# A planned order for a four-layer graph network: transfers planned later than their data, a re-cut tail, and new seeds

## The chip, the cores and the metric

The kernel runs on one core of a Trainium2 chip. The metric is the device time of one execution in microseconds (us). The engines are PE (matrix multiplication; the loading of its weights has a row of its own, PEld), DVE (vector), ACT (scalar, activations), POOL (GpSimd) and SP, which here does nothing but issue DMA transfers. Each engine works through its own list of instructions in order and waits on semaphores for the others.

## The reference

The input is x, 64 graphs of 256 nodes with 128 features (float32), and one 256 x 256 adjacency matrix. Four layers follow one another, and after each the result is added to x and layer-normalized over the features:

```python
# layer 0: five gated recurrent steps; adj @ h is both m_in and m_out
u3 = h @ u3_w.T + u3_b
z = sigmoid(av @ w3_w.T + w3_b + u3);  r = sigmoid(av @ w4_w.T + w4_b + u3)
hv = tanh(av @ w5_w.T + w5_b + (r * h @ u5_w.T + u5_b))
h = (1.0 - z) * h + z * hv
# layer 1: a masked softmax over edges, split into its diagonal and the rest
out = (A * M) @ (x @ W[0]) + (A * (1.0 - M)) @ (x @ W[1]) + bias
# layer 2: graph attention (softmax over masked scores), layer norm, then a GIN block
h_gat = relu(layernorm((softmax(scores) * adj) @ h))
z = relu(layernorm(((1 + eps) * h_gat + adj @ h_gat) @ W1 + b1))
out = relu(z @ W2 + b2 + h_gat)
# layer 3: a polynomial in adj of degree three, with seven weight matrices
y = sum_k (adj^k @ x) @ V_k
```

## The kernel before

The graphs are taken in 32 pairs. A pair's x is one tile of 128 partitions by 512 numbers (two graphs, two blocks of 128 nodes, 128 features). For every pair the program records operations: an engine or a choice of engines, an estimated time for each, what is read, what is written. `pe`, `act`, `dve`, `pool` and `S.add` record; nothing is issued until all 32 pairs are recorded.

`Schedule.order` (from line 164) then plays the whole list through in time, with one clock per engine, and issues the operations in the order of their planned starts. This order is what the chip gets: each engine's list, SP's too, is in that order, and the semaphores only make late data wait. The planner picks, among all operations whose inputs are planned to be there, the one that can start first; on equal starts the one that is most overdue by `late`. Three things in it matter here.

- `SEEN` and `LAG` say how long after an operation's end another engine can see its result. A transfer's own duration is in its `dma` triple: wait, move, after. Loads of x and of transposed x have `XLOAD` and `TLOAD`.
- Buffers are shared by class (`CLASSES`): 15 tiles of class X for x, 4 of class T for transposed x as it is loaded (`hT`), 38 of class A for everything else of this size, 8 PSUM banks and so on. A tile goes back to `free` when its last reader is planned to be done, and the planned start of the next user is not before that. `hT` of a pair is read in the first of the five steps alone, last by the instruction of line 769.
- `SEEDS` holds a number for each window of 15 us of planned time. A number other than 0 shifts the `late` of every operation by a pseudo-random amount, and so deals a different order among operations that compete in this window.

A turn (line 558) transposes a tile through DRAM: DVE transposes blocks of 32 x 32 (line 578), SP writes the tile out (line 580), and SP fetches it back with four transfers (line 586). Each costs SP an issue, and every layer has turns: 315 in all, five of them per pair in layer 0. Lines 595 and 599 are the same for the last step of layer 0. In layer 2 a row of scores goes out and comes back in the same way (lines 853 and 854), `store` (line 908) writes the result, and `load` (line 299) reads x and transposed x for later pairs.

Products with the adjacency are made by `spread7` (lines 628 to 649), which trades an eighth of the multiplications for sums on DVE and POOL; layer 3 has similar forms in `polynomial7` (line 1014) and `spread_on7` (line 1057). Gates of layer 0 are matmuls of 512 columns (lines 746 to 762). At the very end, `plain` and `by_tile` choose forms with shorter chains.

`by_tile` (lines 944 to 968) is layer 3 of the last pair. It multiplies the four blocks of tokens into one bank r, copies r to rr, multiplies four tiles t of their own, adds a2T (adjacency squared) times rr to each, and calls `finish` for tiles 0 and 1 together, then for 2, then for 3. `finish` (lines 970 to 991) takes the mean of squares of a tile (ACT with an accumulator, line 976; for the second tile of a pair DVE, lines 980 and 981), adds epsilon (DVE, line 984), raises to the power -1/2 (POOL, line 985), scales the tile (lines 987 and 988) and stores it (line 991). Means need no subtraction, since the weights are centred beforehand.

Of the kernel before, what the change touches and what calls it, by code (L numbers as in the profile page):

```python
# [9 lines left out]
ALU = mybir.AluOpType  # L10
AX = mybir.AxisListType

P = 128
# [47 lines left out]

SLOW = (1.3, 1.1, 1.4, 0.8)

SEEDS = [0, 113, 303, 1481, 0, 12107, 0, 23552, 32642, 38944, 40117, 45598, 51141, 55839, 63359, 69543, 72829,
         79574, 82143, 87571, 0, 98805, 103528, 113912, 114624, 0, 126288, 133041, 139576, 144350, 0, 153924, 0,
         162906, 171850, 173442, 179398, 188820, 193760, 197487, 201873, 206536, 212282, 216407, 222763, 227951,
         233844, 242079, 243498, 250362, 255262, 263475, 269522, 271926, 278854, 283108, 287499, 292248, 301945,
         304995, 0, 0, 0, 0, 0, 0, 0, 0, 0, 0, 0, 0, 0, 0, 14340575, 14343728, 14346224, 0, 14354974, 0, 14360087,
         14365526, 14369726, 14372687, 0, 0, 14385549, 14386751, 14392959, 14396499, 0, 14402025, 14408122,
         14412300, 14417102, 14417543, 14421809, 14425091, 0]  # L70


def mm(cols, n=1):

    return n * (0.2241 if cols <= 130 else cols * 0.001665 + 0.0065)
# [40 lines left out]
class Schedule:  # L116
# [47 lines left out]
    def order(self, tiles):  # L164

        self.prepare()
        engines = dict.fromkeys([*SEEN, "PORT"], 0.0)
        free = {cls: [(0.0, k) for k in range(len(ts))] for cls, ts in tiles.items()}
        ready, full, moved, out, window = [op for op in self.ops if not op.before], set(), 0.0, [], 0

        def slots(v):
            return [s for s in free[v.cls] if not v.seeded or (v.cls, s[1]) in full]

        while ready:
            best, homes, seed = None, {}, SEEDS[window] if window < len(SEEDS) else 0
            for op in ready:
                held = op.since
                for v in op.holds:
                    if v.home is None:
                        if (v.cls, v.seeded) not in homes:  # L180
                            homes[v.cls, v.seeded] = min((s for s, _ in slots(v)), default=1e9)
                        held = max(held, homes[v.cls, v.seeded])
                if held == 1e9 or best and held > best[0][0]:
                    continue
                way = None
                for engine, us, uses, spare, fn in op.plans:
                    start = max(held, *(engines[e] for e in uses))
                    if way is None or start + us + spare < way[0]:
                        way = start + us + spare, start, engine, us, uses, fn
                late = op.late  # L190
                if seed and op.pair >= 0:
                    late += NUDGE * (1 + seed % 3) * shuffled(op.number, seed)
                    late += GROUP * (seed // 3 % 3) * shuffled(100000 + 4 * op.pair + op.layer, seed)
                key = (way[1], late, op.number)
                if best is None or key < best[0]:
                    best = key, op, way
            if best is None:
                raise RuntimeError("the shared tiles are too few for this order")
            (start, _, _), op, (_, _, engine, us, uses, fn) = best
            if start >= (window + 1) * WINDOW:  # L200
                window += 1
                continue
            ready.remove(op)
            for v in op.holds:
                if v.home is None:
                    slot = min(slots(v), key=lambda s: s[0])
                    free[v.cls].remove(slot)
                    v.home, v.ap = slot[1], tiles[v.cls][slot[1]]
            end, base = start + us, engine.rstrip("+-")
            for e in uses:  # L210
                engines[e] = end
            seen = SEEN[base] + LAG
            if op.dma:
                wait, move, after = op.dma
                moved = max(moved, end + wait) + move * MARGIN
                seen = moved + after - end + LAG
            out.append((start, op.number, op, fn))
            for v in op.holds:
                v.left, v.end = v.left - 1, max(v.end, end + seen)
                if not v.left:  # L220
                    free[v.cls].append((v.end, v.home))
                    (full.add if v.full or v.seeded else full.discard)((v.cls, v.home))
            for x in op.then:
                same = engine != "SP" and x.base == base
                x.waits, x.since = x.waits - 1, max(x.since, end + (AGAIN.get(base, 0.0) if same else seen))
                if not x.waits:
                    ready.append(x)
        self.span = max(engines.values())
        return [(op, fn) for _, _, op, fn in sorted(out, key=lambda x: x[:2])]
# [11 lines left out]
def kernel(ctx: ExitStack, tc: tile.TileContext, x, xT, adj, adjT, mats, cols, rows, out):  # L241
# [11 lines left out]
    def pe(us, fn, r, w):  # L253
        S.add([("PE", us, fn)], r, w)

    def act(us, fn, r, w):
        S.add([("ACT", us, fn)], r, w)
# [289 lines left out]
    def tokens(v):  # L547
        return v.at(4, D)
# [395 lines left out]
    def by_tile(xT, qT, p):  # L944

        r, rr, tiles = bank(), Value("A", name="rr"), []

        def product(t, o, c, k):
            def fn():
                nc.tensor.matmul(o(), tokens(xT)[:, c, :], vx.ap[:, k, :], start=(k == 0 or c == 0), stop=False, skip_group_check=True)  # L950
                nc.tensor.matmul(o(), tokens(qT)[:, c, :], vq.ap[:, k, :], start=False, stop=True, skip_group_check=True)
            pe(mm(128, 2), fn, [xT, qT, vx, vq, *[t] * (k == 1 and c > 0)], [t])

        for c in range(4):
            product(r, lambda c=c: tokens(r)[:, c, :], c, 1)
        evacuate(lambda: rr.at(512), lambda: r.at(512), [r], [rr])
        for c in range(4):
            t = bank()
            product(t, lambda t=t: t.at(D), c, 0)
            tiles.append(t)  # L960
        for group in ((0, 1), (2,), (3,)):
            for c in group:
                def fn(c=c, t=tiles[c]):
                    for j in range(2):
                        nc.tensor.matmul(t.at(D), a2T.ap[:, j, c % 2 * P:(c % 2 + 1) * P], tokens(rr)[:, c - c % 2 + j, :], start=False,
                                         stop=(j == 1), skip_group_check=True)
                pe(mm(128, 2), fn, [a2T, rr, tiles[c], *tiles[max(c - 1, 0):c]], [tiles[c]])
            finish([tiles[c] for c in group], Value("A", name="last"), group[0], p)

    def finish(ts, o, first, p):  # L970

        n, s, st, junk = len(ts), Value("S", name="ms"), Value("S", name="st"), Value("A", name="junk")
        mv = lambda k: s.at(32)[:, 2 * k:2 * k + 2]
        var, rs = (lambda: s.at(32)[:, 1:2 * n:2]), (lambda: s.at(32)[:, 8:8 + n])
        means, outs = [Part(s) for _ in ts], [Part(o) for _ in ts]
        act(0.37, lambda: nc.scalar.activation(junk.at(D), ts[0].at(D), AF.Square, scale=D ** -0.5, accum_out=mv(0)[:, 1:2]),
            [ts[0]], [means[0], junk])

        def by_dve():
            nc.vector.bn_stats(st.at(6), ts[1].at(D))  # L980
            nc.vector.bn_aggr(mv(1), st.at(6))
        if n > 1:
            dve(0.5, by_dve, [ts[1]], [means[1], st])
        dve(0.07, lambda: nc.vector.tensor_scalar(rs(), var(), LN_EPS, None, op0=ALU.add), means, [s])
        pool(0.7, lambda: nc.gpsimd.tensor_tensor(rs(), rs(), neg_half.ap[:, :n], op=ALU.pow), [s, neg_half], [s])
        if n > 1:
            act(0.35, lambda: nc.scalar.mul(o.at(n, D)[:, 0], ts[0].at(D), rs()[:, 0:1]), [ts[0], s], [outs[0]])
        dve(0.3, lambda: nc.vector.tensor_scalar(o.at(n, D)[:, n - 1], ts[n - 1].at(D), rs()[:, n - 1:n], None, op0=ALU.mult),
            [ts[n - 1], s], [outs[n - 1]])
        where = out[2 * p:2 * p + 2].rearrange("b (t p) d -> p (b t) d", p=P)[:, first:first + n]  # L990
        S.add([("SP", 0.52, lambda: nc.sync.dma_start(where, o.at(n, D)))], outs, [], (0.6, 0.25 * n, 0.9))
# [144 lines left out]
```

## Time and profile before

| | us |
|---|---|
| median of three runs | 1469.06 (1468.51 to 1469.07) |
| profiled execution | 1470.28 |
| its span, first to last instruction | 1468.5 |
| PE busy | 1458.2 |
| DVE busy | 1277.1 |
| ACT busy | 1067.8 |
| POOL busy | 990.8 |

The span is 1.8 us shorter than the execution that it belongs to, and that execution is 1.2 us longer than the median. Engine rows are times in which at least one instruction of the engine ran. Matmuls overlap, so PE's row can count a short stall as busy; the distance from one matmul's start to the next is the finer measure. The granted clock of PE is 1.00 in all stretches that the prediction uses. A float32 matmul stands in the trace as two instructions. "SPq" is SP's queue: the time from an issue to the next, or a wait in front of one.

### The profile page before, as it was taken

The page shows a single profiled execution, that of the slowest core. Times are in us where ns is not written, and L with a number is a line of the kernel's source. Part 1 is how long each engine was busy: PE and PEld are TensorE (multiplying, and loading weights), DVE is VectorE, ACT ScalarE, POOL GpSimd, SP SyncE. Part 2 cuts the span into 40 slices and gives each one's busy share as a digit, 9 for nine tenths or more (in the row PEclk, how much of TensorE's full clock was granted, in tenths as well). Part 3 has the DMA queues.
Part 4 walks back from the last instruction along what each step waited for, and adds up shares of the span by engine and source line. Part 5 has one row for each costly group of instructions (what it writes and reads, how often), then busy time and mean ns, then how long its engine had stood idle before and what let it go on. Part 6 is the DMA issues. An engine that isn't in the chain of part 4 may idle for free.

```text
span 1468.5 us, 29324 instructions
## 1 busy us (share of the span) xinstructions
PE 1458.2 (99%) x8188; PEld 1064.8 (73%) x8188; DVE 1277.1 (87%) x3166; ACT 1067.8 (73%) x3277; POOL 990.8 (67%) x1549
## 2 busy tenths in 40 slices
PE   9999999999999999999999999999999999999998
PEld 6555666666677777777676777777777767788998
DVE  7866978988899989989998989888798998999986
ACT  4444555666787988887876677767678787899986
POOL 4432454466677878787684767766677776789764
PEclk9999999999999999999999999999999999999999
DMA  7554455676778898888778575876767878787763
GB/s 228 102 120 95 101 115 130 146 160 148 155 155 173 177 187 177 172 167 162 150 154 164 125 157 127 170 148 136 152 141 169 155 156 161 161 164 168 155 131 75
DMA packets 901283, 219.83 MB, mean 150 GB/s; under 512 B 673280, under 2 KB 892544, under 8 KB 901120
## 3 DMA queue, kind: packets, MB, share of 16 engines
q1 hardware_dynamic: 901120, 217.96, 70.9%
q8 instruction: 66, 1.08, 0.3%
q14 instruction: 97, 0.79, 0.2%
HBM read 118.43 MB, written 99.42 MB: 148 GB/s over the span
## 4 chain that ended last, share of the span: by engine, by line
PE 94%; DVE 2%; POOL 2%; SPq 1%; issue 1%; DMA 0%; ACT 0%; POOLq 0%; DVEq 0%; ACTq 0%
PE ps L628 24%; PE ps L761 9%; PE ps L746 9%; PE ps L762 9%; PE ps L747 9%; PE ps L754 9%; PE ps L784 7%; PE ps L1014 6%; PE ps L884 4%; PE ps L1057 2%; PE ps L844 2%; PE ps L610 1%; PE ps L1040 1%; SPq L586 1%; PE ps L799 0%
## 5 line engine op out<-in xcount | busy, mean ns | idle before, releaser
L628 PEld LDWEIGHTS ps<-aT,a 128*128 128x128 f32 x2192 | 296.3, 192 | 84.0 <-issue 74.4
L274 ACT COPY a<-ps 128x128 f32<-128x128 f32 (+2 forms) x612 | 255.7, 437 | 112.0 <-PE ps L628 52.2
L628 PE MATMUL ps<-aT,a 128*128 128x128 f32 x2192 | 322.6, 275 | 1.1 <-DVE a L634 0.7
L750 ACT ACTIVATE a<-ps,bzrh 128x512 f32<-128x512 f32 x160 | 110.7, 692 | 107.5 <-PE ps L747 103.2
L765 ACT ACTIVATE ps<-ps,bzrh 128x512 f32<-128x512 f32 x160 | 106.6, 666 | 88.5 <-PE ps L762 87.2
L643 POOL TENSOR_TENSOR a<-a 128x256 f32<-128x256 f32 x139 | 107.2, 774 | 93.1 <-ACT a L274 90.4
L761 PE MATMUL ps<-a,w 128*128 128x512 f32 x320 | 163.8, 594 | 0.1
L762 PE MATMUL ps<-a,u5h 128*128 128x512 f32 x320 | 163.4, 592 | 0.0
L747 PE MATMUL ps<-a,w 128*128 128x512 f32 x320 | 163.4, 592 | 0.0
L754 PE MATMUL ps<-a,w 128*128 128x512 f32 x320 | 162.6, 593 | 0.1
L649 DVE TENSOR_TENSOR a<-ps,a 128x256 f32<-128x256 f32 x237 | 98.0, 416 | 73.9 <-PE ps L628 34.5
L707 ACT ACTIVATE a<-ps 128x128 f32<-128x128 f32 x502 | 132.8, 289 | 33.1 <-PE ps L784 21.2
L647 POOL TENSOR_TENSOR a<-a 128x128 f32<-128x128 f32 x206 | 99.6, 489 | 65.4 <-DVE a L643 55.2
L715 POOL TENSOR_TENSOR s<-s,neg_half 128x4 f32<-128x4 f32 x127 | 137.7, 1086 | 6.1
L756 ACT ACTIVATE a<-ps,bzrh 128x512 f32<-128x512 f32 x160 | 110.5, 691 | 39.0 <-PE ps L754 36.3
L784 PE MATMUL ps<-W,a 128*128 128x128 f32 x960 | 135.2, 275 | 0.0
L784 PEld LDWEIGHTS ps<-W,a 128*128 128x128 f32 x960 | 123.7, 192 | 13.8 <-issue 12.0
L746 PE MATMUL ps<-a,W 128*128 128x512 f32 x256 | 131.1, 594 | 0.5 <-DVE a L649 0.5
L578 DVE STREAM_TRANSPOSE a<-a 128x512 f32<-128x512 f32 x185 | 128.2, 698 | 2.5 <-ACT a L727 0.5
L747 PEld LDWEIGHTS ps<-a,w 128*128 128x128 f32 x320 | 60.8, 190 | 76.5 <-issue 67.0
L762 PEld LDWEIGHTS ps<-a,u5h 128*128 128x128 f32 x320 | 60.8, 190 | 76.5 <-issue 64.3
L767 DVE SCALAR_TENSOR_TENSOR ps<-a,ps 128x512 f32<-128x512 f32 x160 | 109.2, 683 | 3.8 <-ACT a L756 2.8
(268 smaller groups left out, 3588.1 us busy)
## 6 DMA issues: line engine op xcount, KB each, us to landing
e<-a SPq DMA_DIRECT2D x283, 256.0 KB
a<-e SPq DMA_DIRECT2D x1132, 64.0 KB
e<-b SPq DMA_DIRECT2D x32, 512.0 KB
b<-e SPq DMA_DIRECT2D x128, 128.0 KB
x<-x_in SPq DMA_DIRECT2D x32, 256.0 KB
t<-xT_in SPq DMA_DIRECT2D x32, 256.0 KB
a<-d SPq DMA_DIRECT2D x32, 256.0 KB
y_out<-a SPq DMA_DIRECT2D x31, 256.0 KB
```

Of the source, the lines that this page charges most:

```text
L274: S.add([("ACT", us[0], lambda: nc.scalar.copy(o(), i())), ("DVE", us[1], lambda: nc.vector.tensor_copy(o(), i()))], r, w)
L578: dve(n / 512 * 0.55 + 0.09, lambda: nc.vector.transpose(st.at(n), i.at(n)), [i], [st])
L628: pe(mm(128), lambda: nc.tensor.matmul(blk(t, k), left(), rt(), start=start, stop=True, skip_group_check=True), [*r, right, terms, *[t] * ...
L707: nc.scalar.activation(tokens(junk)[:, c, :], v.at(len(tiles), D)[:, k, :], AF.Square, scale=D ** -0.5, accum_out=mv()[:, c, 1:2])
L715: pool(1.02, lambda: nc.gpsimd.tensor_tensor(rs(), rs(), neg_half.ap, op=ALU.pow), [s, neg_half], [s])
L746: nc.tensor.matmul(t.at(512), mat("u3"), hT.at(512), start=True, stop=False)
L747: nc.tensor.matmul(t.at(512), w4.ap, mT.at(512), start=False, stop=True)
L750: act(0.59, lambda t=t, r=r: nc.scalar.activation(r.at(512), t.at(512), AF.Tanh, bias=bzrh.ap[:, 1:2], scale=0.5), [t, bzrh], [r])
L754: pe(mm(512), lambda t=t, mT=mT: nc.tensor.matmul(t.at(512), w3.ap, mT.at(512), start=False, stop=True, skip_group_check=True), [w3, mT, t ...
L761: nc.tensor.matmul(t.at(512), w5.ap, mT.at(512), start=True, stop=False)
L762: nc.tensor.matmul(t.at(512), u5h.ap, r.at(512), start=False, stop=True)
L784: nc.tensor.matmul(tokens(t)[:, c, :], tokens(i)[:, c, :], w(), start=(first and k == c == 0), stop=(k == len(lefts) - 1), skip_group_chec ...
```

## The change

Four things are changed.

1. Planning of transfers: an operation of SP that follows another engine's is planned `QUEUED` = 0.5 us later than before.
2. Planning of tiles: a tile of class T counts as free 4.0 us later than its last reader's planned end.
3. `SEEDS` is replaced as a whole (the first two numbers are equal); the order of issue differs throughout.
4. The tail: in `by_tile` the a2T products of tiles 0 and 1 come before the products of tiles 2 and 3, and each later tile's own a2T product comes directly after its product. In `finish` a tile that is alone no longer has its epsilon added by DVE: tiles 2 and 3 have one more column, which a memset sets to sqrt(128 * epsilon), and ACT's sum of squares over 129 columns contains it. The two-tile case is as before, but for the planner's time of the add (0.15 for 0.07).

```diff
+QUEUED, SLACK = 0.5, {"T": 4.0}
...
-SEEDS = [0, 113, 303, 1481, 0, 12107, 0, 23552, 32642, 38944, 40117, 45598, 51141, 55839, 63359, 69543, 72829,
...
+SEEDS = [0, 113, 201, 0, 6923, 12557, 17576, 0, 28432, 33733, 41075, 46356, 54499, 57205, 61367, 69244, 73096,
...
-                    free[v.cls].append((v.end, v.home))
+                    free[v.cls].append((v.end + SLACK.get(v.cls, 0.0), v.home))
...
-                x.waits, x.since = x.waits - 1, max(x.since, end + (AGAIN.get(base, 0.0) if same else seen))
+                more = AGAIN.get(base, 0.0) if same else seen + (QUEUED if x.base == "SP" and base != "SP" else 0.0)
+                x.waits, x.since = x.waits - 1, max(x.since, end + more)
...
-        def product(t, o, c, k):
+        def product(t, o, c, k, after=()):
...
-            pe(mm(128, 2), fn, [xT, qT, vx, vq, *[t] * (k == 1 and c > 0)], [t])
+            pe(mm(128, 2), fn, [xT, qT, vx, vq, *after, *[t] * (k == 1 and c > 0)], [t])
...
         for c in range(4):
             t = bank()
-            product(t, lambda t=t: t.at(D), c, 0)
+            if c > 1:
+                dve(0.1, lambda t=t: nc.vector.memset(t.at(D + 1)[:, D:], (D * LN_EPS) ** 0.5), [rr], [t])
+            product(t, lambda t=t: t.at(D), c, 0, [tiles[-1]] if c > 1 else [])
             tiles.append(t)
-        for group in ((0, 1), (2,), (3,)):
-            for c in group:
-                def fn(c=c, t=tiles[c]):
+            for k in {1: (0, 1), 2: (2,), 3: (3,)}.get(c, ()):
+                def fn(k=k, t=tiles[k]):
                     for j in range(2):
...
-                pe(mm(128, 2), fn, [a2T, rr, tiles[c], *tiles[max(c - 1, 0):c]], [tiles[c]])
-            finish([tiles[c] for c in group], Value("A", name="last"), group[0], p)
+                pe(mm(128, 2), fn, [a2T, rr, tiles[k]], [tiles[k]])
+            if c:
+                finish(tiles[:2] if c == 1 else tiles[c:], Value("A", name="last"), max(c, 2) if c > 1 else 0, p)
...
-        act(0.37, lambda: nc.scalar.activation(junk.at(D), ts[0].at(D), AF.Square, scale=D ** -0.5, accum_out=mv(0)[:, 1:2]),
-            [ts[0]], [means[0], junk])
...
         if n > 1:
+            act(0.37, lambda: nc.scalar.activation(junk.at(D), ts[0].at(D), AF.Square, scale=D ** -0.5, accum_out=mv(0)[:, 1:2]),
+                [ts[0]], [means[0], junk])
...
-        dve(0.07, lambda: nc.vector.tensor_scalar(rs(), var(), LN_EPS, None, op0=ALU.add), means, [s])
+            dve(0.15, lambda: nc.vector.tensor_scalar(rs(), var(), LN_EPS, None, op0=ALU.add), means, [s])
+        else:
+            act(0.37, lambda: nc.scalar.activation(junk.at(D + 1), ts[0].at(D + 1), AF.Square, scale=D ** -0.5, accum_out=rs()),
+                [ts[0]], [s, junk])
```

## The prediction

> **What bounds the kernel now.** I read the page first, then the windows by stage, the waits of PE and of SP, the chain around each PE stall, and the timeline of the end.
>
> ```profile
> span 1468.5 us, 29324 instructions
> PE 1458.2 (99%) x8188; PEld 1064.8 (73%) x8188; DVE 1277.1 (87%) x3166; ACT 1067.8 (73%) x3277; POOL 990.8 (67%) x1549
> PE 94%; DVE 2%; POOL 2%; SPq 1%; issue 1%; DMA 0%; ACT 0%; POOLq 0%; DVEq 0%; ACTq 0%
> ```
>
> PE is busy for all but 10.3 us, and the chain is 94% PE. But a busy PE could hide slack, so I checked its pitch in the chain (start, length, line, count):
>
> ```profile
> 1139.97 0.86 PE ps L746 x2
> ...
> 1443.70 0.89 PE ps L1014 x8
> ...
> 1456.42 1.73 PE ps L936 x8
> ```
>
> Two instructions of 512 columns take 0.86 us, 8 of 128 take 0.89, 8 of 256 take 1.73: pitches of 0.429, 0.1117 and 0.216. The groups by shape count 6284 instructions of 128 or 130 columns, 292 of 256 and 1600 of 512 (12 others are tiny): 6284 x 0.1117 + 292 x 0.216 + 1600 x 0.429 = 1451 us. PE runs at its pitch nearly everywhere, and the change leaves the list of matmuls as it is. So only about 17 us can move. By the starts of the matmul records, where each start-to-start time is set against its pitch, they are: 1.2 before the first matmul, 3.5 more in the first 40 us, 6.5 of stalls between 40 and 1450, 5.3 from the start of the last matmul to the end (the remainder is rounding of the pitches).
>
> The windows show where the 6.5 us lie (columns: window, length, then busy time of PE, PEld, DVE, ACT, POOL, clock, DMA share, GB/s):
>
> ```profile
> 40.00:500.00 460.00, 460.00 (x2187) 299.50 (x2186) 385.56 (x864) 294.85 (x773) 259.00 (x417) 1.00 0.65 135
> 500.00:600.00 100.00, 99.12 (x604) 75.36 (x603) 88.93 (x244) 86.62 (x286) 80.40 (x122) 1.00 0.86 175
> 1100.00:1200.00 100.00, 99.36 (x567) 72.17 (x566) 91.74 (x221) 80.92 (x256) 74.23 (x117) 1.00 0.80 162
> 1300.00:1400.00 100.00, 98.29 (x692) 88.90 (x691) 94.52 (x288) 93.47 (x358) 82.31 (x115) 1.00 0.79 160
> ```
>
> From 40 to 500 PE never stops. Start to start the stalls are 1.8 us at 548 to 570, 1.85 at 1107 to 1184 and 2.75 at 1330 to 1400. Their causes differ. The first is a late transfer; its chain runs through the SP queue, back to back, to a tile that lands late, then POOL:
>
> ```profile
> 550.43 1.90 SPq L586
> 556.63 2.10 DMA a<-e
> 558.80 0.74 POOL a L634
> ```
>
> The other two have no transfer at their root. At 1155 DVE and POOL sit on each other: DVE L643, 0.42 us at its usual length, starts in its record at 1155.14 and is through only at 1158, when POOL's last sum ends:
>
> ```profile
> 1155.14 2.97 DVE L643 TENSOR_TENSOR a<-a 128x256 f32<-128x256 f32 x2 [0.21 <-ACT a L274]
> ...
> 1156.74 0.74 POOL L1004 TENSOR_TENSOR a<-a 128x256 f32<-128x256 f32 x1
> ```
>
> At 1396 POOL runs L1005, L1004, L1006 and then the L634 for which PE waits 1.6 us. So 1.8 of the 6.5 us belong to transfers, 4.7 to engines.
>
> SP's own waits, which the new planning aims at (total, times, longest):
>
> ```profile
> SPq L580 <- DVE a L578: 149.4, 92, 8.0
> SPq L586 <- DMA e<-a: 52.3, 39, 3.5
> SPq L299 <- DVE a L769: 39.8, 13, 11.3
> ```
>
> SP stands still for hundreds of us, and PE hardly notices: prefetch and many pairs in flight hide it.
>
> **The change part by part.**
>
> *The tail.* Today, in the last pair, 16 products of r run from 1457.98, 16 of the tiles from 1459.77, 16 with a2T from 1461.55 to 1463.34 (0.1117 each). The finish is then:
>
> ```profile
> 1463.51 1.73 POOL L985 TENSOR_TENSOR s<-s,neg_half 128x2 f32<-128x2 f32 x3 [2.44 <-DVE s L984]
> 1463.54 0.28 ACT L976 ACTIVATE a<-ps 128x128 f32<-128x128 f32 x1
> 1463.71 0.20 ACT L976 ACTIVATION_READ_ACCUMULATOR a<-ps 128x1 f32 x1
> ...
> 1465.28 0.35 DVE L988 TENSOR_SCALAR a<-ps,s 128x128 f32<-128x128 f32 x1 [0.17 <-POOL s L985]
> ```
>
> Three powers in a row on POOL (0.70, 0.52, 0.53) set the end: the last one's input is there at 1464.09, but POOL is free only at 1464.73. The new order puts a2T of tiles 0 and 1 before the products of 2 and 3: 8 instructions, 0.89 us, earlier. The first group's power then begins about 0.9 us earlier, at 1462.61 (with its add as now), and ends at 1463.31; tile 2's ends at 1463.83. The last tile's matmuls still end at 1463.34, its square at 1463.91. The removed DVE add (L984, 0.15 and the hand-over) brings the last power to 1463.97, its end to 1464.50, the scaling to 1464.52 to 1464.87, against 1465.63: 0.76 earlier. What follows (SP issue and landing, 2.9 to the span's end) stays. The cover at risk: a2T of tile 0 now comes 0.89 earlier, at 1460.66, and its input, ACT's copy of r, ends at 1460.55. That is 0.1 of room; behind a waiting a2T the whole rest of PE's work queues, so a copy that starts 0.5 later costs 0.4. And ACT runs six L727 until 1462.25, which can hold the first square; that would put the last power 0.15 later. I take 0.7, ends 0.2 and 0.8. The two new memsets of one PSUM column are not in this trace: between 0.06 (the memset of neg_half) and 0.35 (L988) each, in DVE's idle 2.68 us before L980, so nothing; uncovered they delay the square of tile 2, which has 0.3 of room before POOL takes it. A square of 129 columns for 128 is nothing.
>
> *Half a microsecond before SP issues.* 381 issues follow an engine's result: 283 + 32 first halves of a turn, 32 score lines, 34 stores. Each is planned 0.5 us later, and what reads the turned tile with it. No instruction is added; the queue's order and the margin change. 92 waits on L578 average 1.6 us, so 0.5 shortens the blocking in front of the queue by up to 46 us of SP time, and PE's consumers get about 0.5 more room. The only transfer stall begins with 0.48 us of lateness (558.2) and pulls 1.3 more after it through DVE and POOL. I take all of it, 1.8; the ends are 0 and 1.8. Each pair has 12 such steps, so it lives some 6 us longer in the plan; some 15 pairs in flight hide that. Without that cover it would cost up to 6 once, at the end.
>
> *Four microseconds for tiles of transposed x.* 28 of 32 loads reuse one of four tiles. From the eighth load on the issue precedes the first matmul that reads it by 65 to 255 us, so four is nothing. But the fifth to seventh go out at 22.4, 23.7 and 36.4 for matmuls at 37.6, 39.8 and 42.3: leads of 15.2, 16.0 and 6.0. I take nothing, because PE has pairs 0 to 3 to work on; the upper end is 4 for each of two turnovers, 8. The SP time it saves (39.8 us of blocking) lies at 25 and 44 for the most part, where PE is full: nothing.
>
> *New seeds, a new order.* The 4.7 us that engines cause are dealt anew. Nothing in the change speaks to them, so I take them as unchanged; ends: 0 and twice as much. The start: the first two seeds (0 and 113) are unchanged, and no early load follows a computed value, so 0.
>
> [...]
>
> Sum against the profiled execution (1470.28, span 1468.5, 1.8 around it): -0.7 - 1.8 = -2.5, so a span of 1466.0. That execution is 1.2 above the median of 1469.06; the same difference gives **1466.6**. 0.2%, 2.9 us, is about what a measurement of this kernel can tell from no change.
>
> **Rivals.**
> 1. *Nearly every stall goes.* For it: 460 us in a row without one. Against: two of three places have no transfer in them. All 6.5 and the tail give 1461.9; with an eighth or so left, 1463.
> 2. *The transfers were hidden anyway.* SP's 149 us of waits cost PE 0.3 us directly ("PE ps L628 <- DMA a<-e: 0.3, 1, 0.3" is among PE's waits), and a new order makes another late tile. Only the tail counts: 1468.4.
> 3. *The start starves (slower).* The loads at 22 to 36 us go out 4 us later, and pairs 4 to 6 with them; the next generation 4 more. If PE has nothing else in 20 to 120 us, it loses 8: 1469.06 - 0.7 + 8 = 1476.4. It decides from 3.6 us uncovered. For: a lead of 6.0. Against: PE full there with SP blocked for 11.3 us at 25.
> 4. *Transfers pass each other badly (slower).* A first half that is planned later falls behind another tile's four fetches (L586, 0.55 each, 2.2). Less the 0.5 of room, PE loses 1.7 each time; four such among 315 turns make 1469.06 - 0.7 + 6.8 = 1475.2. It decides from the third. For: the DMA share of 0.86 at 500 to 600. Against: one such case today.
>
> **How the numbers follow.** Forecast 0.37 (own range 1465.0 to 1468.2), rivals 0.22, 0.17, 0.12 and 0.12. Faster than 1466.1: a third of the forecast (0.12) and rival 1 (0.22), 0.34. Slower than 1472.0: rivals 3 and 4, 0.24. Within: 0.42. The range goes from just under rival 1 to rival 3, 1462.5 to 1476.5, which leaves the full end of rival 1 and more than 8 us of loss outside, some 2 in 10.
>
> **What would show it.** Right: the last L985 starts within 0.1 us of its square's end, the last scaling 1.2 to 1.4 us after the last a2T instruction; "SPq L580 <- DVE a L578" well under 149; no PE wait on a transfer. PE at 100% in 40 to 120 speaks against rival 3. Wrong: stalls over 10 us between 40 and 1450, on whatever engine they end; or PE idle over 6 us in the last 20, if pairs came to the end in another order.

## The result and the profile after

The changed kernel takes **1478.55 us** (median of six runs, 1476.45 to 1480.64) against 1469.07 (six runs, 1468.18 to 1469.82): a ratio of 1.0064, interval 1.0053 to 1.0074. It is slower, outside the range of 1462.5 to 1476.5. Its profiled execution took 1477.63, with a span of 1475.9, 7.4 above that of before. The page of the changed kernel:

```profile
span 1475.9 us, 29402 instructions
PE 1460.9 (99%) x8188; PEld 1064.6 (72%) x8188; DVE 1283.8 (87%) x3154; ACT 1061.4 (72%) x3284; POOL 1007.2 (68%) x1559
```

The matmuls are the same 8188, so all 7.4 us are stalls or ends. Set start to start against the pitch, as in the prediction, they are:

| us of stall | 0 to 40 | 40 to 100 | 500 to 600 | 700 to 800 | 1000 to 1200 | 1200 to 1300 | 1300 to 1400 | 1400 to 1450 | all | last matmul's start to end |
|---|---|---|---|---|---|---|---|---|---|---|
| before | 2.84 | 0.13 | 1.79 | -0.03 | 1.66 | 0.10 | 2.71 | -0.01 | 8.98 | 5.28 |
| after | 2.77 | 2.13 | 1.34 | 0.75 | 0.97 | 0.24 | 8.12 | 0.37 | 16.52 | 5.09 |

(The stretches that are left out hold -0.2 in all in both; values below 0.15 are rounding of the pitches. The prediction's figures for before, 3.5 up to 40 us and 6.5 from there to 1450, come out here as 2.8 and 6.1.) 7.54 of stalls less 0.19 at the tail make the 7.35. The same stages in the windows of after (columns as in the prediction's fence):

```profile
40.00:100.00 60.00, 58.12 (x211) 33.20 (x210) 50.99 (x98) 26.17 (x47) 27.09 (x46) 1.00 0.50 106
500.00:600.00 100.00, 99.32 (x615) 76.08 (x615) 93.62 (x255) 84.03 (x276) 82.81 (x119) 1.00 0.88 175
1100.00:1200.00 100.00, 99.51 (x566) 71.79 (x565) 90.67 (x223) 77.21 (x248) 76.33 (x119) 1.00 0.75 153
1300.00:1400.00 100.00, 94.70 (x657) 83.58 (x657) 93.60 (x271) 87.10 (x333) 77.72 (x109) 1.00 0.79 163
```

Two stages carry the loss: 40 to 100, where PE of before was full, and 1300 to 1400, where its busy time falls from 98.29 to 94.70. The granted clock is 1.00 in all four. Lines of after are numbered three to eight higher (L583 is the old L580, L753 the old L750). Waits of PE in after:

```profile
PE ps L757 <- ACT a L753: 2.9, 3, 1.9
PE ps L813 <- DVE ps L807: 1.5, 1, 1.5
PE ps L613 <- DVE x L682: 1.0, 1, 1.0
PE ps L631 <- DVE a L772: 0.8, 1, 0.8
PE ps L750 <- DVE a L652: 0.7, 1, 0.7
```

No row of this list names a transfer any more; the "DMA a<-e" of before is gone. But SP waits longer, not shorter:

```profile
SPq L583 <- DVE a L581: 171.6, 91, 20.4
SPq L589 <- DMA e<-a: 71.6, 47, 4.1
```

A wait of PE names only the last releaser. Followed back in time, the chain that ends PE's stall at 1370 to 1372 in after leaves PE at 1311 and comes back to it only at 1372 (start, length, what ran):

```profile
1318.90 4.26 DMA a<-d
...
1349.54 2.50 DMA e<-a
...
1352.11 1.99 DMA a<-e
...
1361.64 1.33 POOL s L673
1363.00 0.16 DVE s L675
1363.16 1.03 DVE x L682 x4
1364.19 0.06 DVE a L894
1364.25 0.46 issue
1364.70 0.42 DVE a L1014
1365.12 0.63 DVE a L581
1365.77 2.33 DMA e<-a
1368.14 0.03 issue
1368.17 2.42 DMA a<-e
1370.60 1.23 DVE b L581
1371.83 0.39 DVE ps L807
1372.26 1.13 PE ps L813 x4
```

So a normalisation, a turn out and back through DRAM (4.8 us) and the step on its result follow each other without slack, and another turn (1349) and a fetched row of scores (1318) stand further up in the same chain: in this stretch the latency of the pairs that are left sets PE's pace. In before the same view leaves PE from 1319 to 1338 and from 1383 to 1398, through ACT, DVE and POOL; no transfer stands in it.

The tail of after:

```profile
1467.94 2.29 ACT L730 ACTIVATE a<-ps,s 128x128 f32<-128x128 f32 x8
...
1469.99 1.06 PE L969 MATMUL ps<-a,a2T 128*128 128x128 f32 x8
1470.10 0.30 ACT L991 ACTIVATE a<-ps 128x129 f32<-128x129 f32 x1
...
1470.63 0.28 ACT L982 ACTIVATE a<-ps 128x128 f32<-128x128 f32 x1
...
1471.53 1.22 POOL L993 TENSOR_TENSOR s<-s,neg_half 128x1 f32<-128x1 f32 x2 [0.41 <-ACT a L991]
```

The square of the first group (L982) comes after that of tile 2 (L991), and two powers still follow each other on POOL.

### The profile page after: what moved, and what is told of

It is laid out like the page before. It is cut to its first block, busy times and chain, and to the rows that moved or that the text cites. A ratio compares the mean times of both kernels' runs of the same rounds, so it can differ in the third digit from the quotient of the medians.

```text
span 1475.9 us, 29402 instructions
## 1 busy us (share of the span) xinstructions
PE 1460.9 (99%) x8188; PEld 1064.6 (72%) x8188; DVE 1283.8 (87%) x3154; ACT 1061.4 (72%) x3284; POOL 1007.2 (68%) x1559
## 5 line engine op out<-in xcount | busy, mean ns | idle before, releaser
L277 ACT COPY a<-ps 128x512 f32<-128x512 f32 (+2 forms) x613 | 255.4, 436 | 124.0 <-PE ps L631 54.9
L753 ACT ACTIVATE a<-ps,bzrh 128x512 f32<-128x512 f32 x160 | 110.4, 691 | 101.2 <-PE ps L750 91.8
L750 PE MATMUL ps<-a,w 128*128 128x512 f32 x320 | 163.5, 592 | 0.7 <-DVE a L652 0.7
L646 POOL TENSOR_TENSOR a<-a 128x256 f32<-128x256 f32 x136 | 103.4, 762 | 88.7 <-ACT a L277 87.7
L750 PEld LDWEIGHTS ps<-a,w 128*128 128x128 f32 x320 | 60.6, 190 | 77.8 <-issue 68.2
```

The lines of the kernel that those rows point to most:

```text
L277: S.add([("ACT", us[0], lambda: nc.scalar.copy(o(), i())), ("DVE", us[1], lambda: nc.vector.tensor_copy(o(), i()))], r, w)
L750: nc.tensor.matmul(t.at(512), w4.ap, mT.at(512), start=False, stop=True)
```

## The experiments

Three theories were open. *The plan's end*, formed after the result: planning half a microsecond later lengthens the last pairs' chains when there is nothing else to do, the cost that the prediction said other pairs hide. *The order of the transfers*: SP's new list makes transfers late. *The deal*: the seeds put other work in front of what PE needs, whatever the two planning changes do. "Planned" below is the planner's own arithmetic, made before anything is issued. All ratios are to the kernel before, run on the same chip.

**The tail alone.** Before's order and seeds; `by_tile` and `finish` are those of the change (a constant on `late` of the last pair keeps the rest of the order as it was).

```diff
-            op.late = self.due(op.pair) - op.rest + HOLD[op.layer] if op.pair >= 0 else -1e4
+            op.late = self.due(op.pair) - op.rest + HOLD[op.layer] + (0.4482 if op.pair == self.n_pairs - 1 else 0.0) if op.pair >= 0 else -1e4
```

> The order of before, instruction for instruction, up to the last pair's by_tile, with the new by_tile and finish alone. The prediction's term for the tail was -0.7 us. Theory: the profile of the changed kernel shows eight L730 on ACT in front of the first tile's square, so the first group's power comes last on POOL and only 0.2 us of the 0.7 are left: 1468.9, distance from the last matmul's start to the end 5.1 (before 5.28). Rival: the ordering of the tail gains all of it here, since ACT's older work is that of another order: 1468.4 and 4.6.

Measured 1469.42, ratio 1.0004 (0.9995 to 1.0013): no gain, and above both times that were forecast. From the last matmul's start to the end it takes 5.53 (before 5.28). A variant in which DVE takes the statistics of both tiles of the first group:

```diff
-            act(0.37, lambda: nc.scalar.activation(junk.at(D), ts[0].at(D), AF.Square, scale=D ** -0.5, accum_out=mv(0)[:, 1:2]),
-                [ts[0]], [means[0], junk])
...
+            for k in range(2):
+                def by_dve(k=k):
+                    nc.vector.bn_stats(st.at(2, 6)[:, k, :], ts[k].at(D))
+                    nc.vector.bn_aggr(mv(k), st.at(2, 6)[:, k, :])
+                dve(0.5, by_dve, [ts[k]], [means[k], st])
```

> As x1_tail (the order of before with the new tail), but DVE, which is idle there, takes the statistics of both tiles of the first group, so that no square of it waits behind ACT's scaling of the pair before. If that scaling is why the new tail gained nothing: the last power is tile 3's, start of the last matmul to the end 4.5 in place of 5.5 (x1_tail) and 5.3 (before), 1468.2. If the tail gains nothing for another reason: as x1_tail, 1469.4.

Measured 1468.77, ratio 0.9997 (0.9988 to 1.0006); the tail is 4.74. That looked like ACT's fault, but DVE's longer statistics also changed the planner's order on PE. The issue order shows it: in the tail alone, and in after, the planner issues a2T of tile 1, product and a2T of tile 2, product of tile 3, and only then a2T of **tile 0** (the row of eight L969 at 1469.99 above is tile 0's four and tile 3's four). In the variant tile 0's a2T comes before the product of tile 3. Two more kernels tell the causes apart: one edge that enforces the order the code is written in, without and with DVE's statistics.

```diff
-            product(t, lambda t=t: t.at(D), c, 0, [tiles[-1]] if c > 1 else [])
+            product(t, lambda t=t: t.at(D), c, 0, tiles[c - 2:] if c > 1 else [])
```

> Before's order and the new tail, with one more edge: the product of tile 2 waits for the a2T products of tiles 0 and 1, as the prediction assumed that the new order would have it. Theory A (the planner issued tile 0's a2T products behind tile 3's product, and that ate the gain): the first group's square starts within 0.2 us of the end of ACT's six scalings, its power is no longer after those of tiles 2 and 3, and the time from the last matmul's start to the end falls from 5.53 in the tail alone to 4.7 (before: 5.28); by the prediction's own term, -0.7, it would be 4.6. Theory B (ACT's scalings of the pairs before hold the squares, whatever PE's order): it stays at 5.3 to 5.5. Median by A 1468.8, by B 1469.4.

> The same edge, and DVE takes the statistics of both tiles of the first group, so that ACT's scalings cannot hold them. If ACT's hold is the smaller part, the time from the last matmul's start to the end is within 0.15 us of that with the edge alone (4.6 to 4.7); if it is the larger part, it falls by 0.5 or more below it. Median 1468.2 to 1468.8; no part of it can make the kernel slower than before by more than 0.5.

Measured: with the edge 1469.00, ratio 0.9997 (0.9988 to 1.0006), tail 4.90; with DVE's statistics too 1468.48, ratio 0.9995 (0.9986 to 1.0004), tail 4.83. The edge alone gives 0.63 of the 0.79 between the tail alone and the variant, and DVE's statistics add 0.07 to it, so PE's order is the larger part. It missed the 4.7 because POOL now waits: the sum for the first group is there at 1460.63, but POOL takes tile 2's power first.

```profile
1460.04 0.29 ACT L979 ACTIVATE a<-ps 128x128 f32<-128x128 f32 x1
...
1460.46 0.17 DVE L986 TENSOR_SCALAR s<-s 128x2 f32<-128x2 f32 x1 [0.21 <-ACT a L979]
...
1461.07 1.73 POOL L990 TENSOR_TENSOR s<-s,neg_half 128x1 f32<-128x1 f32 x3 [2.08 <-ACT a L988]
```

These are the fastest kernels of the study, but none is told from before by its interval.

**SP's list alone.** Before's plan; only the order in which SP's issues are written out is shifted, first by 0.5 and 4.0, then by 1.5 and 4.0.

```diff
+QUEUE = 0.5, 4.0
...
-        return [(op, fn) for _, _, op, fn in sorted(out, key=lambda x: x[:2])]
+        def issued(x):
+            start, number, op, _ = x
+            if op.base == "SP":
+                start += QUEUE[0] if any(b.base != "SP" for b in op.before) else 0.0
+                start += QUEUE[1] if op.holds and op.holds[0].cls == "T" and op.pair > 3 else 0.0
+            return start, number
+        return [(op, fn) for _, _, op, fn in sorted(out, key=issued)]
```

> The plan of before, its seeds and every engine's order; only SP's list is sorted anew, with each transfer that follows an engine's result 0.5 us later and each reload of a tile of transposed x 4 us later, which moves 45 issues past another. So it holds what the change does to the queue on the chip, without what it does to the plan. If the queue is what costs (transfers pass each other badly): 1472 or more, PE waiting on tiles that land late. If the queue's order was hidden and the loss comes from the plan: 1469.1, within 1.5. If later issue helps as the prediction had it, the stall of 1.8 us at 548 to 570 goes: 1467.3.

> As x2_queue, with 1.5 us in place of 0.5: some 160 issues change places. If the queue costs, three times the shift costs more than x2, 1475 or above. If prefetch and the pairs in flight hide the queue: 1469 to 1471. If later issue helps: at or under x2.

Measured 1470.32, ratio 1.0012 (1.0002 to 1.0021), for half a microsecond, and **1513.77**, 1.0303 (1.0288 to 1.0319), for 1.5: 45 us. In the first 45 issues change places. Its profile has 0.8 more stall at 40 to 100, 0.9 more in the 500s and 1.1 less in 1000 to 1200; the time is nearest to the theory that the queue's order is hidden, and the gain that later issue was to bring (1467.3) did not come. The second stalls in every stage, 17.4 us of it in 100 to 500. SP's waits of the second show why:

```profile
SPq L594 <- DMA e<-a: 228.1, 126, 4.1
```

Before it was 52.3 in 39 waits. A first half that is moved back lands next to its own four fetches; SP then waits in front of them until it has landed, up to 4.1 us, and everything behind waits with it. Rival 4's mechanism exists, then, at a shift of 1.5; at 0.5 the loss was 1.5 us (1470.32 against 1468.81 of before on the same chip). The reverse is a run with after's plan, in which SP's list is sorted as if neither delay were planned (85 issues change places):

```diff
+            if op.base == "SP":
+                start -= QUEUED if any(b.base != "SP" for b in op.before) else 0.0
+                start -= SLACK["T"] if op.holds and op.holds[0].cls == "T" and op.pair > 3 else 0.0
```

> The changed kernel's plan and every engine's order, with SP's list sorted anew as if transfers were not planned later: 0.5 us earlier after an engine's result, reloads of transposed x 4 us earlier (85 places change). If issuing later costs on the chip whatever the plan (x2_queue lost 1.5, x3_queue2 45): 1476 to 1477. If it costs only where the readers are not planned later with it, and here they are: 1478.5 within 1.

Measured 1478.51, ratio 1.0066 (1.0053 to 1.0080): nothing changes, with the same 2.10 us lost at 40 to 100 and 7.94 in 1300 to 1400. The order of SP's issues is not what makes the changed kernel slow.

**One planning change at a time.** The new tail throughout. A plan with seeds that were not fitted to it ends 35 to 60 us later, so each got seeds of its own by the same search: none of the two changes, 0.5 alone, the four microseconds alone, both.

```diff
-QUEUED, SLACK = 0.5, {"T": 4.0}
+QUEUED, SLACK = 0.0, {}
```

> The planning of before (no delay for transfers, no slack for tiles) with the new tail, and with other seeds, chosen window by window for the least idle PE in the plan; the plan ends at 1483.2 where before's ends at 1482.0 and after's at 1484.5. If the new planning is what costs, an order dealt anew under the old one stays near before: 1470, between 1467 and 1473. If it is the luck of the deal, whatever the planning, this lands as far off as after does: over 1475, with stalls of 5 us or more beyond before's between 1300 and 1450.

> The 0.5 us alone, without the slack for tiles, with the new tail and my own seeds from the first window on. The plan ends at 1507.1 with 38 us of idle after 1300, as s1 (40.4, measured 1494.8) and b1 (40.6, 1491.0). If the plan's holes decide: 1489 to 1495; between 40 and 1300 at most 1 us of stalls.

> The slack of 4 us for tiles of transposed x alone, without the 0.5 us, with the new tail and seeds of my own from the first window on (found as for n1). The plan ends at 1508.6, 25 over n1's 1483.2, with nearly all of its holes after 1400. Rival 3 of the prediction (the start starves) wants 2 us or more of stalls between 40 and 100, as in after (2.1), where before has 0.1. If the loss of after at 49 us is an order in which the set-up of layer 1 runs early, none here: its softmax stands at 157 us in this plan, at 49 in after's. The whole: 1495 to 1500 if the plan's holes are real.

> Both planning changes with the new tail, as in after, with seeds of my own from the first window on in place of after's (found as for n1). The plan ends at 1509.3, after's at 1484.5. If the two planning changes cost nothing on the chip and only the plan is pessimistic, this comes close to n1 (1473.9), 1480 at most. If the plan's holes are real: 1495 to 1500. Between 40 and 100: as for s1, since the softmax stands at 123 us.

Measured, in this order: 1473.88 (ratio 1.0033, 1.0021 to 1.0045), 1488.24 (1.0132, 1.0113 to 1.0150), 1494.82 (1.0175, 1.0154 to 1.0195), 1491.01 (1.0149, 1.0129 to 1.0169). The first is the deal alone: neither planning change, other seeds, and 4.8 us slower than before by its ratio, with 8.6 us of stalls after 1300. It lies between its two forecasts, under 1473 and over 1475. The last three plans were bad at the end: their last pair is planned to start 35 to 39 us later than in before, and with both changes this search ended at 1509.3 where after's seeds end at 1484.5. So these times don't price the changes. But their stages do tell something. The middle of the kernel with both changes:

```profile
40.00:100.00 60.00, 60.00 (x221) 34.54 (x220) 43.70 (x80) 26.87 (x45) 24.86 (x44) 1.00 0.44 94
100.00:1300.00 1200.00, 1200.00 (x6674) 859.05 (x6673) 1048.17 (x2559) 882.75 (x2671) 862.04 (x1334) 1.00 0.74 152
```

No stall from 40 to 1300, start to start either. Neither planning change need cost anything there; what after loses before 1300 comes from how its order was dealt. And the four microseconds alone starve nothing at the start:

```profile
40.00:100.00 60.00, 60.00 (x221) 34.59 (x220) 44.80 (x81) 27.06 (x46) 25.25 (x44) 1.00 0.50 104
```

**The end by itself.** To price half a microsecond where few pairs are left, the plans of before and of after are kept to their 1230th microsecond, and the rest is planned with 0.5 or without it, each with its own seeds (a second set as a measure of the search's scatter).

```diff
+SWITCH, LATER = 82, 0.0
...
-                more = AGAIN.get(base, 0.0) if same else seen + (QUEUED if x.base == "SP" and base != "SP" else 0.0)
+                more = AGAIN.get(base, 0.0) if same else seen + ((QUEUED if window < SWITCH else LATER) if x.base == "SP" and base != "SP" else 0.0)
```

> The plan of before up to 1230 us with the new tail, then seeds of my own as for a01, no 0.5 us. Planned idle after 1300 is 14.1 against 9.4 for before's own seeds. If the chip follows the plan's idle: 1473.5, 4.7 over before. If a stage up to 1230 with fewer stalls is what counts: 1469 to 1470.

> As b01 with the 0.5 us from 1230 on. Planned idle after 1300 is 19.8. If the chip follows the plan's idle: 1479, 5 to 6 over b01. If not: as b01 within 1.5.

> b01 once more with other seeds after 1230 us: the scatter of the deal at the same plan before it. Planned idle of PE after 1300 is 15.7 (b01 14.1, which measured 1470.1 and 4.4 us of stalls after 1300). If the chip follows the plan's idle, at the rate of bq1 against b01 (3.7 us for 5.7): 1471.1. If it is luck: anywhere from 1468 to 1478.

> The changed kernel's plan up to 1230 us; from there transfers are planned without the 0.5 us, with seeds of my own for the last windows (800 tried for each, the least idle PE in the plan is kept). Planned idle of PE after 1300: 14.0, as in after (14.0; before 9.4). If what thins the end is the idle that the plan itself holds: about as after, 1478, with 8 us of stalls from 1300. If the 0.5 us hurts on the chip in another way (transfers that are issued late): 1473 or less, stalls as in before (2.7).

> The same with the 0.5 us kept to the end, same number of seeds tried. The plan's idle after 1300 is 18.3, 4.3 more than a01's. If the chip follows the plan's idle: 4 to 5 us slower than a01. If the half microsecond is only in the plan and real transfers come as early as ever: the same as a01 within 1.5.

> a01 once more with other seeds after 1230 us: the changed kernel's plan up to there, no 0.5 us after it. Planned idle after 1300 is 19.8 (a01 14.0, which measured 1477.8 with 8.9 us of stalls there). If the plan's idle decides: 4 us over a01, 1482. If what was dealt before 1230 decides: 1477 to 1479 again, and in any case 2.1 us of stalls between 40 and 100 as in after.

| first 1230 us | from there | planned end | idle of PE planned after 1300 | stalls measured after 1300 | median | ratio (interval) |
|---|---|---|---|---|---|---|
| before | as before | 1482.0 | 9.4 | 2.7 | 1469.07 | 1 |
| before | no 0.5 | 1485.3 | 14.1 | 4.5 | 1470.07 | 1.0007 (0.9997 to 1.0016) |
| before | no 0.5, other seeds | 1486.0 | 15.7 | 7.3 | 1471.61 | 1.0020 (1.0011 to 1.0030) |
| before | 0.5 | 1490.6 | 19.8 | 8.2 | 1473.74 | 1.0031 (1.0018 to 1.0043) |
| after | as after | 1484.5 | 14.0 | 8.5 | 1478.55 | 1.0064 (1.0053 to 1.0074) |
| after | no 0.5 | 1482.7 | 14.0 | 9.0 | 1477.76 | 1.0058 (1.0043 to 1.0073) |
| after | no 0.5, other seeds | 1488.4 | 19.8 | 8.4 | 1478.48 | 1.0063 (1.0048 to 1.0078) |
| after | 0.5 | 1487.8 | 18.3 | 11.5 | 1482.11 | 1.0084 (1.0069 to 1.0099) |
| none of the two (above) | | 1483.2 | 16.0 | 8.6 | 1473.88 | 1.0033 (1.0021 to 1.0045) |
| 0.5 alone (above) | | 1507.1 | 38 | 23.4 | 1488.24 | 1.0132 (1.0113 to 1.0150) |
| 4.0 alone (above) | | 1508.6 | 40.4 | 32.9 | 1494.82 | 1.0175 (1.0154 to 1.0195) |
| both (above) | | 1509.3 | 40.6 | 28.0 | 1491.01 | 1.0149 (1.0129 to 1.0169) |

Two things follow. First, with equal search, half a microsecond in the last 250 us costs 1473.74 - 1470.07 = 3.7 on before's first part and 1482.11 - 1477.76 = 4.4 on after's; the plans had said 5.3 and 5.1. The scatter of the search is 1.5 and 0.7, so against the second seeds it is 2.1 and 3.6. The stalls on the chip grow with the idle that the plan itself holds, but loosely, from three to eight tenths of it. That this idle alone decides was forecast twice and missed: 1473.5 for before's first part without 0.5 (1470.07), 1482 for after's with other seeds (1478.48). A single profile's stalls scatter too: the order of after gives 8.5 after 1300 here and 8.3 and 12.3 in two more runs, the one with SP's list sorted back (above) and the one with ten operations moved at 49 us (below). Second, after's first 1230 us cost more than that: with no 0.5 behind either, 1477.76 and 1478.48 against 1470.07 and 1471.61, 7.3 us on average. Between the profiles of the first pair, 7.3 apart, 3.2 are stalls before 1300 (2.1 at 49 us and 0.75 at 799 among them), and 4.5 are larger stalls behind, 9.0 against 4.5 at the same planned idle of 14, less 0.4 at the tail. Up to 1.7 of the 4.5 is a halved clock (last section). These 1230 us hold the new seeds and both planning changes together; what they hand on that makes the end worse than planned is not settled. In after itself the end counts for less than in its split run with 0.5: its own seeds are 3.6 better there (1478.55 against 1482.11), and taking the 0.5 out with newly searched seeds gave only 0.8 (1477.76).

**The stall at 49 us.** In after's plan the set-up of layer 1, a softmax over the adjacency, is dealt to 49 us (in before to 157). PE waits for gate L753, and ACT has an exponential of the set-up ahead of it:

```profile
48.63 0.67 DVE L439 TENSOR_REDUCE s<-a 128x2 f32<-128x512 f32 x1
...
49.34 0.51 ACT L441 ACTIVATE a<-a,s 128x256 f32<-128x256 f32 x1 [3.76 <-DVE s L439]
...
50.34 1.24 ACT L753 ACTIVATE a<-ps,bzrh 128x512 f32<-128x512 f32 x2
...
51.06 1.12 PE L757 MATMUL ps<-a,w 128*128 128x512 f32 x2 [1.88 <-ACT a L753]
```

ACT stands idle for 3.76 us in front of work that layer 1 does not need for over 100 us, with the gate behind it in the list. A run with these ten operations issued 2 us later in after's order:

```diff
+            return start + (DELAY if 40.0 < start < 60.0 and op.number in HELD else 0.0), number
```

> The changed kernel with one stretch of its order altered: ten operations of layer 1's set-up (the softmax of the adjacency, planned at 49 to 57 us) are issued 2 us later, so that ACT runs the gate of pair 5 ahead of the two exponentials in place of behind them. If ACT's order is what makes PE wait 2.05 us at 49: stalls between 40 and 100 go from 2.1 to 0.1, and the whole to 1476 (2.1, and some more where the stall had also halved PE's clock). If PE has no work there because tiles of transposed x come later (rival 3): it waits just as long for the next thing, 1478.5.

Measured 1478.23, ratio 1.0067 (1.0053 to 1.0081). The stall fell from 2.13 to 1.16, and the whole did not become faster: a new stall of 0.7 at 56 us, and 10.7 us in 1300 to 1400 in its profile. That execution took 1481.17, 2.9 above the median, and its clock was halved for 3.4 us (mean of the execution 0.998) behind a stall of 2.87 at 1324, where after lost 0.82. The cause of the stall at 49 us is confirmed; that the whole would follow is a miss.

## Why the prediction was wrong

- *The tail, -0.7.* In after it gave 0.19, alone -0.25. The failing step is "The new order puts a2T of tiles 0 and 1 before the products of 2 and 3". That is the order of the code; the planner issued tile 0's a2T behind tile 3's product. Of the hint "ACT runs six L727 until 1462.25, which can hold the first square" the sum took 0.15; after has eight of them, and the first group's square at 1470.63. With the order enforced the tail gives 0.38, and 0.45 with ACT out of the way too, inside the ends of 0.2 and 0.8. In the ten kernels with searched seeds the planner put tile 0's a2T before tile 3's product, and the last matmul's start to the end took 4.18 to 4.81, so 0.5 to 1.1 less than before; the term was sound where the order held. The memsets and the wider square cost nothing, as said: in after the two memsets are 0.07 us in one row at 1465.42 and end 4.6 us before the first square that reads them, and a square of 129 columns takes 288 ns (mean of two), one of 128 278.
- *New seeds, 4.7 unchanged, ends 0 and twice as much.* This is the step that failed by most: "Nothing in the change speaks to them, so I take them as unchanged". Stalls between 40 and 1450 went from 6.1 to 13.7, with no transfer as the last releaser of any, more than the upper end. A softmax dealt to 49 us costs 2.1, and with the same end planned in the same way after's first 1230 us cost 7.3 more than before's. The prediction treated a new deal as neutral around a mean; but before's deal was a good one, with little idle planned at the end (9.4), and after's plan holds 14.0. The deal alone cost 4.8 in the kernel with neither planning change.
- *Half a microsecond, -1.8.* The failing step is "some 15 pairs in flight hide that. Without that cover it would cost up to 6 once, at the end". There is no such cover in the last 250 us, and the cost there is 2.1 to 4.4 on the split plans, about the size of the whole forecast gain of 2.5. The prediction had the price and left it out of the sum and of the rivals. The gain of 1.8 is not shown by any run. The kernel with both changes and other seeds has no stall in the 500s, but neither has the one with neither change. And the stall itself was in good part an accident of the profiled execution: seven other kernels have before's order, instruction for instruction, up to 1230 us of the plan, and theirs is 0.45 to 0.96 (a row stands below). The sum took 1.8 from an execution that was 1.2 above the median and then subtracted that 1.2 as well. PE waits for no transfer directly, as said; but SP's 149.4 us of waits, which should have fallen well under that, became 171.6.
- *Four microseconds for tiles, 0.* Nothing contradicts it: no stall in 40 to 100 with them alone. Rival 3 named a time near the result (1476.4) and even the place, but its mechanism is not what happened: the 2.1 us there are a softmax in ACT's list. What the four microseconds cost at the end was not told apart.
- *Rival 4* is real as a mechanism (45 us with 1.5) and not the cause: the changed kernel without the shifts in SP's list takes as long.
- *The sign of being wrong* that the prediction named, "stalls over 10 us between 40 and 1450, on whatever engine they end", is what is seen.

The 500s in the kernel with the tail alone, where before has PE busy for 99.12:

```profile
500.00:600.00 100.00, 99.62 (x610) 75.76 (x610) 90.10 (x247) 87.28 (x288) 81.07 (x125) 1.00 0.87 178
```

The row at 1155 is a matter of the execution. With the same lists the first L643 took 2.6 us (2.63 in before) in four of eight executions and 0.42 in the other four, and 1000 to 1200 held 1.6 to 2.0 us of stall in those and 0.4 to 0.6 in these. So this stall is not fixed by the order of the lists; that DVE and POOL hold each other up there was read from that one row, and no run isolates it.

Of the 9.5 us between the medians the two profiles hold 7.35: 1.7 before 1300 (2.0 at 49 us and 0.8 at 799, less 1.1 in the 500s and in 1000 to 1200, where before's profile was higher than most of its kin), 5.8 behind, and -0.2 at the tail. Of the 5.8, the 0.5 at the end has between 0.8 and 4.4; how the rest divides between what the first 1230 us hand on and the seeds behind them is open. The other 2.1 lie in which executions were profiled: before's was 1.2 above its median, after's 0.9 below.

## What to carry to other kernels

Where an order is planned, read the plan's own idle time before costing an edit to it: over twelve kernels the stalls on the chip at the end were three to eight tenths of it, though plans with equal idle still differed by up to 4.9 us. A margin on every hand-over cost nothing here while many pairs were in flight (no stall from 40 to 1300 with both changes) and was paid in the last stage (3.7 and 4.4 us on the split plans); price that stage by itself. One profile is one execution: before a stall of 2 us goes into a sum, see whether a second execution of the same order has it. And check an edit's order in the issued lists, not in the source: a list scheduler moved one tile's matmuls behind those of two others and took the gain.

## What the runs showed of the hardware

Behind a stall of 2 to 3 us PE's granted clock fell to half in some executions and stayed at 1.00 in others. With after's first 1230 us and other seeds behind them (the row "after, no 0.5, other seeds"), the same stall at 49 us was followed by this:

```profile
50.00:52.00 2.00, 1.05 (x3) 0.58 (x4) 1.97 (x5) 1.94 (x5) 1.67 (x4) 0.99 0.00 0
52.00:56.00 4.00, 4.00 (x12) 1.94 (x11) 3.55 (x12) 1.19 (x2) 0.87 (x2) 0.58 0.00 0
56.00:60.00 4.00, 4.00 (x12) 1.85 (x11) 3.51 (x7) 1.81 (x4) 1.21 (x3) 1.00 0.00 0
```

In 52 to 56 the mean clock is 0.58, so it is halved for 3.4 us of it, and 40 to 100 loses 3.82 instead of 2.13. In after itself the same stall leaves the clock at 1.00 over the same 4 us:

```profile
52.00:56.00 4.00, 4.00 (x15) 2.19 (x14) 3.90 (x13) 2.17 (x5) 0.76 (x1) 1.00 0.00 0
```

The run without 0.5 on after's first part shows it at 1368.1 behind a stall of 2.97, that with 0.5 at 1357.6 behind stalls of 0.96 and 1.36 close together; the mean clock of 1300 to 1400 is 0.98 in both. At 49 us the halved clock came with 1.7 us on top of the stall (3.82 less 2.13). So a hole near the end can cost, by an estimate from that, up to 1.7 us on top of itself, and not in every execution. The halved clock isn't the cause of the result: the mean granted clock of after's six executions is 0.999 or 1.000.
